# Node one-hots from broadcast key rows on ScalarE instead of TensorE, and layer-3 target scores made a block ahead, in a four-layer graph network

## The chip, the cores and the metric

The kernel runs on one core of one Trainium2 chip. The metric is the device time of one execution in microseconds. The core has a matrix engine (TensorE, PE in the profile, with its weight loads as PEld), two elementwise engines (VectorE, DVE; ScalarE, ACT), GpSimd (POOL), which here issues the indirect DMAs, and SyncE (SP), which issues the plain DMAs. Each engine works through its own queue in order; semaphores tie the queues together.

## The reference, cut to what matters

6250 nodes with 256 features, 100000 edges sorted by target. Four graph layers follow each other, each added to its input and normalised over the features:

```python
edge_index = jnp.stack([src, dst])
x = _layernorm(x + _L0_gnn_ref(x, edge_index, ...))     # mean of neighbours, two matrices
x = _layernorm(x + _L1_gnn_ref(x, src, dst, ...))       # attention, 8 heads: q[row] . k[col], softmax per source
x = _layernorm(x + _L2_gnn_ref(x, edge_index, ...))     # two GAT layers, 4 heads
x = _layernorm(x + _L3_gnn_ref(x, edge_index, ...))     # mean of neighbours, two matrices
```

The attention layer and the GAT layer are the two that the change touches:

```python
s = jnp.einsum('ehd,ehd->eh', q[row], k[col])
p = jnp.exp(s - m[row])
out = jax.ops.segment_sum((p / denom[row])[:, :, None] * v[col], row, num_segments=n)
...
e = jax.nn.leaky_relu(alpha_s[src] + alpha_d[dst], 0.2)
ex = jnp.exp(e - m[dst])
out = jax.ops.segment_sum(h[src] * alpha[:, :, None], dst, num_segments=n)
```

`q[row]`, `alpha_d[dst]` take a node's row out to its edges, and `segment_sum` brings the edges' rows back to their node. Both are matrix products with one-hot matrices: a node-by-edge hot to go out, an edge-by-node hot to come back.

## The kernel before, in words

The nodes are cut into NB = 50 blocks of B = 125. For each block the edges whose target (or source, in the attention layer) lies in it are laid out in CM = 16 chunks of 128 edges (CAP = 2048 in all); what doesn't fit goes to SH = 2 chunks that 25 blocks share. `key_d` and `key_s` hold for each edge its node's number inside its block, one column a chunk; `idx_d` and `idx_s` hold the other end.

The program has a preparation (to about 200 us) and five passes over the blocks. Pass 1 is the first layer and, beside it, the sort by source. Pass 2 is the attention layer (`piece1`, `finish1`), passes 3 and 4 are the two GAT layers (`piece2`, `finish2` with `layer` 0 and 1), pass 5 is the last layer. Beside passes 3 and 4 `count_edges` builds a table of edge counts for pass 5, one step after most turns.

A block is worked through in four pieces of four chunks, 200 pieces a pass. A piece is a Python generator that issues some instructions and yields the name of a group. `Turns` steps the generators: in each turn it goes through the groups in a fixed order and steps every item of that group that is due; `yield "x"` makes it due in the next turn, `yield "+x"` in this one, if that group is still to come. This order is the order of the instructions in the queues of PE, DVE and ACT. POOL and SP are not ordered by hand.

Pass 2, a piece: gathers of four chunks of `kv_table` into `g` (7 buffers), POOL. Then "tp": TensorE makes both hots. `by_node` and `by_key` are factors of 56 rows whose product is 1 minus the squared distance of node and key; four products give `t_t` (node by edge), one gives `t_s` (edge by node), both in the bank `tp`. Then "act": ScalarE evicts them through a Relu, to `ts` in bf16 (L1873) and to `st` in f32 (L977, `positive`). Then "qe" (L1882): `ts` times the three bf16 parts of the block's `q` gives each edge its query. Then "prod" (L1889): keys times queries on DVE, a reduction `s` (L1821), and two Exp on ACT (L1825 to `iota_p`, L1826 to `msg`). Then "msg" (L1828): values times weights on DVE. Then "ps" (L1908): `st` times `msg` is summed in the block's bank. After its last piece a block goes through `finish1`: the division, two small transposes and a product (L915, L920, L928), the layer norm (`norm`, L898) and `features`, which multiplies by the GAT weights, stores a row of `hs_table` for each node and keeps the target's score in three bf16 parts, `ad_parts`.

Passes 3 and 4, a piece: gathers of `hs_table` into `g` (9 buffers), POOL; DVE makes the edge-by-node hot `st` by comparison (`one_hots`, L941). "tp": TensorE transposes it (L2085). "act": ScalarE evicts it to `ts` in bf16 (L2088). "pe": `ts` times `ad_parts` of the block gives each edge its target's score, into the one bank `pe` (L2093). "e": the sum `e` (L2049) and the leaky ReLU `r` (L2043) on DVE, two Exp on ACT (L2052, L2053). "msg" (L2055) and "ps" (L2127) as before. `finish2` does the division, Gelu (L2011, another activation table than Exp), then `features` for the next GAT layer, or the norm and the tables of pass 5.

The counting step k makes a hot `a_hot` on DVE (L1965), multiplies that of step k-1 on TensorE into the one bank `a_acc` (L1975) and lets ScalarE evict that of step k-2 to `a_row` (L1951).

## Time and profile before

| what | value |
|---|---|
| median of 3 runs (lowest, highest) | 6354.93 us (6344.74, 6355.41) |
| the profiled execution's own time | 6347.38 us |
| its span on the core | 6345.5 us |
| PE busy in 1410 to 2790 us (pass 2) | 1037.08 of 1380 us |
| PE busy in 2790 to 4160 us (pass 3) | 1028.08 of 1370 us |
| PE busy in 4160 to 5560 us (pass 4) | 957.16 of 1400 us |
| ACT busy in the same three stretches | 386.43, 450.35, 492.35 us |
| POOL busy in the same three stretches | 767.78, 778.13, 757.95 us |

A group of the profile is named by its line, engine, operation and tiles, with its number of instructions, its busy time, the mean length of one, and the idle time of the engine just before it with what ended that idle time. Three passes of 1380, 1370 and 1400 us make two thirds of the span; the change lies in these. The rows of the groups that it takes away, from the groups by shape:

```profile
L2085 PE MATMUL tp<-ident,st 128*125 128x128 f32 x1600 | 308.5, 314 | 40.6 <-issue 30.1 <-DVE st L941 10.1
L2088 ACT CAST ts<-tp 125x512 bf16<-125x512 f32 x400 | 233.3, 583 | 820.7 <-remote 479.2 <-PE tp L2085 164.0 <-PE pe L2093 135.6
L1873 ACT ACTIVATE ts<-tp 125x512 bf16<-125x512 f32 x200 | 118.4, 592 | 258.5 <-PE fin L970 108.1 <-remote 86.4 <-PE tp L1869 37.7
L977 ACT ACTIVATE st<-tp 128x500 f32<-128x500 f32 x200 | 116.5, 582 | 4.6 <-PE tp L970 1.5 <-PE tp L1869 1.4 <-PE qe L1882 0.8
L1869 PE MATMUL tp<-by_key,by_node 56*128 56x128 bf16 x800 | 81.2, 224 | 7.9 <-ACT ts L1873 6.8 <-ACT by_key L966 0.8 <-issue 0.3
L970 PE MATMUL tp<-by_node,by_key 56*128 56x500 bf16 x200 | 78.3, 392 | 22.8 <-ACT by_key L966 18.3 <-issue 4.2 <-ACT st L977 0.2
```

### The profile page before, as it was taken

To read this page: it belongs to the slowest core of one execution; us is meant where nothing else is said; L and a number is where in the kernel's file an instruction comes from. 1 tells how busy PE (TensorE), PEld (TensorE's weight loads), DVE (VectorE), ACT (ScalarE), POOL (GpSimd) and SP (SyncE) were. 2 spreads that over 40 slices of the span, in tenths; PEclk is the share of its full clock that TensorE was granted. 3 is DMA by queue.
4 is the path that set the end of the run, shared out by engine and by line. 5 is a ranking of instruction groups with operands and counts; after the bars stand their busy time and mean duration, and the time that the engine had idled before them with its cause. 6 is when DMAs were issued, how large, how long until landed. Compare 5 with 4: busy or idle time off the path is not lost.

```text
span 6345.5 us, 85961 instructions
## 1 busy us (share of the span) xinstructions
PE 4651.2 (73%) x28778; PEld 3328.7 (52%) x28778; DVE 3995.7 (63%) x11239; ACT 2312.8 (36%) x6308; POOL 3590.8 (57%) x3709
## 2 busy tenths in 40 slices
PE   1567888867777777757777777747766776779996
PEld 0445666645555555535555555535545555545554
DVE  7786666646777777746666666646767767623233
ACT  4016677932322222213333333323333333323332
POOL 5776666645555555535555555455555555455554
PEclk9778999988999999978888888878888878889997
DMA  5555555545655556533333333333333333377774
GB/s 152 152 163 157 160 157 151 153 129 170 177 173 171 172 167 174 171 86 96 105 102 102 102 101 101 90 83 102 104 100 104 105 102 97 93 189 206 205 193 122
DMA packets 383758, 862.39 MB, mean 136 GB/s; under 512 B 85018, under 2 KB 208376, under 8 KB 383304
## 3 DMA queue, kind: packets, MB, share of 16 engines
q0 software_dynamic: 221184, 670.83, 39.0%
q1 hardware_dynamic: 162120, 185.97, 10.2%
q8 instruction: 228, 3.74, 0.2%
q14 instruction: 226, 1.85, 0.1%
HBM read 769.69 MB, written 86.78 MB: 135 GB/s over the span
## 4 chain that ended last, share of the span: by engine, by line
PE 35%; DVE 22%; issue 13%; another core or an unknown queue 10%; ACT 9%; POOL 5%; DMA 3%; SPq 0%; DVEq 0%; ACTq 0%; POOLq 0%
PE ps L2127 6%; PE d L2274 6%; POOL g L932 5%; PE ps L985 5%; PE a_acc L1975 4%; DVE msg L2055 3%; PE po L928 2%; DVE s L1821 2%; PE tp L2085 2%; DVE msg L1828 2%; PE acc L1519 2%; DVE a_hot L1965 2%; DMA g<-kv_table_f,idx_s 2%; PE pt L928 2%
## 5 line engine op out<-in xcount | busy, mean ns | idle before, releaser
L932 POOL DMA_INDIRECT g<-hs_table_f,idx_d x1600 | 1520.9, 951 | 1249.8 <-DVE msg L2055 493.8
L932 POOL DMA_INDIRECT g<-kv_table_f,idx_s x784 | 746.7, 952 | 548.9 <-issue 204.2
L932 POOL DMA_INDIRECT g<-h_table_f,idx_d x800 | 799.5, 999 | 430.6 <-issue 213.8
L2127 PE MATMUL ps<-msg,st 128*125 128x260 f32 x3200 | 919.6, 434 | 97.2 <-DVE msg L2055 52.9
L2127 PEld LDWEIGHTS ps<-msg,st 128*125 128x125 f32 x3200 | 688.5, 218 | 291.6 <-issue 82.8
L1975 PE MATMUL a_acc<-a_hot,a_st 128*128 128x500 f16 x1650 | 497.6, 444 | 373.6 <-ACT a_row L1951 282.8
L2055 DVE TENSOR_TENSOR msg<-g,iota_p 128x1024 f32<-128x1024 f32 x400 | 488.2, 1221 | 403.6 <-ACT iota_p L2052 328.0
L932 POOL DMA_INDIRECT g<-x_table_f,idx_d x416 | 395.7, 951 | 383.4 <-PE ps L985 191.4
L985 PE MATMUL ps<-g,st 128*128 128x256 bf16 (+1 forms) x3648 | 519.3, 293 | 126.1 <-issue 60.4
L985 PEld LDWEIGHTS <-st 128*128 128x128 bf16 x4104 | 419.2, 104 | 255.8 <-issue 150.3
L2088 ACT CAST ts<-tp 125x512 bf16<-125x512 f32 x400 | 233.3, 583 | 820.7 <-remote 479.2
L1965 DVE TENSOR_SCALAR a_hot<-a_nodes,a_ends 128x500 f16<-128x500 f16 x1650 | 505.2, 372 | 18.1 <-remote 18.1
L1908 PE MATMUL ps<-msg,st 128*125 128x264 f32 x1600 | 437.7, 419 | 100.6 <-DVE msg L1828 73.3
L1975 PEld LDWEIGHTS <-a_st 128*128 128x128 f16 x1650 | 180.5, 109 | 577.1 <-issue 484.6
L1908 PEld LDWEIGHTS ps<-msg,st 128*125 128x125 f32 x1600 | 301.4, 199 | 237.3 <-DVE msg L1828 103.9
L941 DVE TENSOR_TENSOR st<-iota_p,key_d 128x500 f32<-128x500 f32 (+1 forms) x550 | 409.8, 746 | 20.8 <-ACT iota_p L2052 16.3
L2274 PE MATMUL d<-cnt,xs 125*128 125x500 bf16 x1800 | 401.2, 378 | 16.9 <-issue 16.5
L1889 DVE TENSOR_TENSOR prod<-g,qe 128x512 f32<-128x512 f32 x400 | 262.3, 684 | 197.5 <-PE qe L1882 68.3
L2049 DVE TENSOR_TENSOR e<-g,pe 128x16 f32<-128x16 f32 x400 | 65.1, 163 | 454.7 <-remote 352.1
L1882 PE MATMUL qe<-q,ts 125*128 125x256 bf16 x2400 | 318.9, 286 | 29.0 <-DVE prod L1889 24.2
L2085 PE MATMUL tp<-ident,st 128*125 128x128 f32 x1600 | 308.5, 314 | 40.6 <-issue 30.1
L1532 ACT ACTIVATE oa<-t_f,blk 125x128 f16<-125x128 f16 x800 | 310.7, 388 | 74.4 <-remote 48.1
(453 smaller groups left out, 8768.0 us busy)
## 6 DMA issues: line engine op xcount, KB each, us to landing
g<-hs_table_f,idx_d POOLq DMA_INDIRECT x1600
xs<-x_table_f SPq DMA_DIRECT2D x75, 336.0 KB
a_table_f<-a_row SPq DMA_DIRECT2D x50, 328.1 KB
few<-a_table_f SPq DMA_DIRECT2D x75, 218.8 KB
g<-h_table_f,idx_d POOLq DMA_INDIRECT x800
g<-kv_table_f,idx_s POOLq DMA_INDIRECT x784
hs_table_f<-hs SPq DMA_DIRECT2D x100, 115.5 KB
own<-hs_table_f SPq DMA_DIRECT2D x100, 115.5 KB
```

The costliest lines, as they stand in the source:

```text
L932: nc.gpsimd.indirect_dma_start(out=g, out_offset=None, in_=table, in_offset=bass.IndirectOffsetOnAxis(ap=idx, axis=0))
L941: nc.vector.tensor_tensor(st, iota_p[:, None, :w].to_broadcast([P, n, w]), key[:, :, None].to_broadcast([P, n, w]), op=ALU.is_equal,)
L985: nc.tensor.matmul(ps[:, :m], st[:, i, :], g[:, i, k * D : k * D + m], start=(c0 + i == 0 and k == 2), stop=(c0 + i == CH - 1 and k == 0),)
L1532: nc.scalar.activation(oa[:, i, :], o1[:, i, :], AF.Copy, scale=val_a[:, at])
L1882: nc.tensor.matmul(qe[:, i, :], ts[:, i0 + i, :], q[:, k * D : (k + 1) * D], start=(k == 0), stop=(k == 2))
L1908: nc.tensor.matmul(sums[b][:B, : D + H1], hot, m[:, i * H1 : (i + 1) * H1, :].rearrange("p h c -> p (h c)"), start=(c == 0), stop=(c == CH ...
L1965: nc.vector.tensor_scalar(hots[k][:, i, :], nodes, ends[:, s, c : c + 1], float(-r * RW), op0=ALU.subtract, op1=ALU.is_equal,)
L1975: nc.tensor.matmul(accs[s, r], sts[s][:, c, :], hot[:, i, :], start=(c == c0), stop=(c == c1 - 1))
L2055: nc.vector.tensor_mul(msg[:, : n * H2, :C2].rearrange("p (n h) c -> p n h c", h=H2), g[:, :n, :D].rearrange("p n (h c) -> p n h c", h=H2) ...
L2085: nc.tensor.transpose(tp[:, i, :], st[:, i, :], ident)
L2127: nc.tensor.matmul(sums[b][:B, : D + H2], hot, m[:, i * H2 : (i + 1) * H2, :].rearrange("p h c -> p (h c)"), start=False, stop=(c == CH - 1),)
L2274: nc.tensor.matmul(accs[h][q], xs[:, i, j * D + h * P : j * D + (h + 1) * P], cnt[:, i, q * RW : (q + 1) * RW], start=(s + i == 0 and j == 2),
```

## The change

Key rows: the preparation and the sort by source store the keys of each block as one row of 2048 bf16 numbers in DRAM, `keys_d` and `keys_s`. In passes 2 to 4 SP loads a block's row to all 125 partitions at once (`load_keys`, three buffers), six turns ahead of the block's first piece. From three turns ahead ScalarE turns it into the node-by-edge hot where it lies, a quarter a turn: Square with minus the partition's number as bias, then Relu of 1 minus that (`node_hots`). So `by_node`, `by_key`, their products, the transposes `tp` and the copies `ts` go.

Pass 2's edge-by-node hot is made by ScalarE too (`edge_hots`): a Square for each chunk, with the key as bias, and one Relu for the piece, when the piece is made. In passes 3 and 4 it stays with VectorE.

Passes 3 and 4: the scores of a block's targets are made for the whole block, with the hots, into one of two banks `pe`; the piece only reads them. A piece takes two stages fewer. The order of the groups changes, `run_pass` also adds the key generators, `qe` gets four banks, `ps` three in pass 2, `g` six buffers in passes 2 to 4, and the counting gets a step more between its product and its eviction, with a third `a_hot` and a second `a_acc`.

```diff
+        minus = const.tile([P, 1], F32, name="minus")
+        nc.gpsimd.iota(minus, pattern=[[1, 1]], base=0, channel_multiplier=-1, allow_small_or_imprecise_dtypes=True)
...
+        keys_d, keys_s = (dram.tile([NB, CAP], BF16, name=f"keys_{k}_f") for k in "ds")
...
+        def node_hots(kb, q):
+
+            part = kb[:, q * 4 * P : (q + 1) * 4 * P]
+            nc.scalar.activation(part, part, AF.Square, bias=minus[:B])
+            nc.scalar.activation(part, part, AF.Relu, bias=ones[:B, 0:1], scale=-1.0)
+
+        def edge_hots(work, key, n, most, bufs, name):
+
+            st = work.tile([P, most, B], F32, name=name, bufs=bufs)[:, :n, :]
             for i in range(n):
...
+                nc.scalar.activation(st[:, i, :], iota[:, :B], AF.Square, bias=key[:, i : i + 1], scale=-1.0)
+            nc.scalar.activation(st, st, AF.Relu, bias=ones[:, 0:1], scale=-1.0)
             return st
...
+            k_rows = pool.tile([NB, CAP], BF16, name="k_rows")
+            nc.scalar.copy(k_rows, k_f)
+            nc.sync.dma_start(out=keys_d, in_=k_rows)
...
+        LEAD_K = 6
+
+        def run_pass(turns, makers, beside=None, keys=None):
...
             for t, make in enumerate(makers):
+                if keys and (t + LEAD_K) % per == 0 and 2 <= (t + LEAD_K) // per < NB:
+                    turns.add(keys((t + LEAD_K) // per))
                 turns.add(make())
...
+        def load_keys(rows, b):
+            kb = keys_pool.tile([B, CAP], BF16, name="kb")
+            move(nc.sync, kb, rows[b : b + 1, :].to_broadcast([B, CAP]))
+            return kb
...
-            turns = Turns(("act", "prod", "msg", "fin", "ps", "late", "qe", "tp", "new"))
+            turns = Turns(("late", "keys", "qe", "prod", "msg", "fin", "ps", "new", "act"))
...
+            def keys1(b):
+                kb = load_keys(keys_s, b)
+                held[b] = work.tile([B, 3 * D], BF16, name="q", bufs=3)
+                move(nc.sync, held[b], block_rows(q_table, b))
+                by_key[b] = kb.rearrange("p (c e) -> p c e", e=P)
+                yield "3keys"
+                for q in range(CM // 4):
+                    node_hots(kb, q)
+                    yield "keys"
...
-                yield "tp"
-                ks = by_key[b]
-                t_t, t_s = (psum.tile([P, 512], F32, name="tp", bufs=2) for _ in range(2))
-                for i in range(n):
-                    nc.tensor.matmul(t_t[:, i * P : (i + 1) * P], by_node[:, c0 + i, :], ks, start=True, stop=True)
-                hots_product(t_s, by_node, ks, c0, n)
-                yield "act"
-                ts = work.tile([B, 4, P], BF16, name="ts", bufs=3)
-                nc.scalar.activation(ts[:, :n, :].rearrange("p c e -> p (c e)"), t_t[:B, : n * P], AF.Relu)
-                st = positive(work, t_s, n, 4, 5, "st")
+                st = edge_hots(work, key_s[:, b, c0 : c0 + n], n, 4, 6, "st")
+                if last:
+                    st_s = edge_hots(work, key_s[:, b, CM:], SH, SH, 2, "st_s")
                 yield "qe"
...
-            for k in range(len(steps) + 2):
-                if k >= 2:
-                    s, r = steps[k - 2]
+            for k in range(len(steps) + 3):
+                if k >= 3:
+                    s, r = steps[k - 3]
...
-                    hots[k] = ap.tile([P, most, RW], F16, name="a_hot", bufs=2)
+                    hots[k] = ap.tile([P, most, RW], F16, name="a_hot", bufs=3)
...
-                    accs[s, r] = apsum.tile([P, 512], F32, name="a_acc")[:, :RW]
+                    accs[s, r] = apsum.tile([P, 512], F32, name="a_acc", bufs=2)[:, :RW]
...
-                turns = Turns(("act", "e", "msg", "fin", "ps", "late", "pe", "tp", "new"))
+                turns = Turns(("late", "keys", "e", "pe", "msg", "fin", "ps", "new", "act"))
...
+                def keys2(b):
+                    kb = load_keys(keys_d, b)
+                    yield "3keys"
+                    ts = kb.rearrange("p (c e) -> p c e", e=P)
+                    pe = scores_d[b] = psum.tile([P, CM, H2], F32, name="pe", bufs=2)
+                    for q in range(CM // 4):
+                        node_hots(kb, q)
+                        yield "+pe"
+                        for c in range(4 * q, 4 * q + 4):
+                            for k in range(3):
+                                nc.tensor.matmul(
+                                    pe[:, c, :], ts[:, c, :], ad_parts[:, b, k, :], start=(k == 0), stop=(k == 2)
+                                )
+                        yield "keys"
...
-                    st = one_hots(work, key_d[:, b, c0 : c0 + n], n, 4, 8)
-                    yield "tp"
-                    tp = psum.tile([B, 4, P], F32, name="tp", bufs=2)
-                    for i in range(n):
-                        nc.tensor.transpose(tp[:, i, :], st[:, i, :], ident)
-                    yield "act"
-                    ts = work.tile([B, 4, P], BF16, name="ts", bufs=3)
-                    nc.scalar.copy(ts[:, :n, :], tp[:, :n, :])
-                    yield "pe"
...
+                    st = one_hots(work, key_d[:, b, c0 : c0 + n], n, 4, 6)
+                    yield "2e"
+                    pe = scores_d[b][:, c0 : c0 + n, :]
...
-                    run_pass(turns, [(lambda a=a: piece2(*a)) for a in made], beside_2)
+                    run_pass(turns, [(lambda a=a: piece2(*a)) for a in made], beside_2, keys2)
```

A digit ahead of a group's name, as in "3keys", means that many turns later. `finish1`, `finish2` and `features` keep their instructions in the new groups: the layer products of a block come first in a turn ("late"), ScalarE's copies of them last ("act"); `features` in pass 2 uses the block's own bank in place of a bank `fin`. The generator for the shared chunks waits five turns in place of four.

## The prediction

> **What bounds the kernel now.** I read the page's busy line first, then busy time by stretch (PE, PEld, DVE, ACT, POOL busy; clock; DMA share; GB/s), because the change touches passes 2 to 4 only. One steady stretch of each:
>
> ```profile
> PE 4651.2 (73%) x28778; PEld 3328.7 (52%) x28778; DVE 3995.7 (63%) x11239; ACT 2312.8 (36%) x6308; POOL 3590.8 (57%) x3709
> ...
> 1600.00:2600.00 1000.00, 768.08 (x4458) 553.35 (x4456) 744.64 (x1449) 291.49 (x823) 575.52 (x605) 0.96 0.59 171
> 3000.00:4000.00 1000.00, 784.30 (x4877) 566.00 (x4877) 658.93 (x1803) 346.31 (x956) 584.55 (x616) 0.87 0.38 102
> 4360.00:5360.00 1000.00, 699.44 (x4462) 515.36 (x4461) 696.91 (x1999) 364.49 (x967) 551.70 (x581) 0.83 0.37 102
> ```
>
> No engine is full: the busiest, PE, idles a fifth to a third of the time. So the engines wait for one another. The waits by stretch (waiting line, releaser, us, times, longest) say where; these are pass 2, then pass 3:
>
> ```profile
> DVE msg L1828 <- issue: 57.0, 84, 2.1
> DVE msg L1828 <- ACT iota_p L1825: 46.6, 66, 3.0
> DVE prod L1889 <- PE qe L1882: 44.8, 34, 3.9
> DVE prod L1889 <- PE tp L970: 22.9, 18, 1.4
> ACT ts L1873 <- PE fin L970: 94.6, 21, 4.9
> ```
>
> ```profile
> DVE msg L2055 <- ACT iota_p L2052: 149.1, 101, 3.7
> DVE e L2049 <- remote: 114.6, 35, 8.0
> ACT ts L2088 <- remote: 194.7, 35, 12.3
> ACT ts L2088 <- PE pe L2093: 90.6, 18, 7.5
> PE a_acc L1975 <- ACT a_row L1951: 84.1, 62, 3.9
> POOL g L932 <- DVE msg L2055: 196.5, 69, 5.9
> ```
>
> (The last two are from 2900 to 4100 us.) VectorE waits for TensorE's products and for ScalarE's exponentials, and ScalarE's exponentials stand behind copies of one-hots that wait for TensorE. "remote" ahead of `ts` and `e` I take for TensorE as well: nothing but TensorE feeds `ts`, and some matmul records are missing. POOL is held back by VectorE, not the reverse. A stretch of the timeline of pass 3 shows the knot:
>
> ```profile
> 3614.82 0.10 PEld L2093 LDWEIGHTS <-ts 125*128 125x128 bf16 x1
> 3616.11 0.15 DVE L2049 TENSOR_TENSOR e<-g,pe 128x16 f32<-128x16 f32 x1
> 3616.32 0.44 PE L2093 MATMUL pe<-ad_parts,ts 125*128 125x4 bf16 x12 [1.11 <-DVE e L2049]
> 3616.60 0.51 PEld L2085 LDWEIGHTS tp<-ident,st 128*125 128x125 f32 x4
> ```
>
> `pe` has one buffer, so the next piece's `pe` waits for `e`, and the transposes `tp` stand behind it.
>
> **What the Trainium skill says.** "TensorE: Matmul & The Clock Gate", Step-by-step: what each phase is for: matmuls stay in program order, only weight loads are pulled ahead. The trace agrees: the load of `ts` at 3614.82 ran 1.5 us before its matmul. "ScalarE: Activation LUTs", What ACT_TABLE_LOAD costs: 186 + 0.833 N ns for an ACTIVATE, about 93 more for each per-partition operand, neighbours overlapping by about 93. The trace agrees: one such operand on 128 elements took 388 ns (L1532; 280 + 107), two on 256 took 600 ns (L898; 585). Same page, Table sets: cheap functions lie in every set; Square is not in that list, though Precision budgets groups it with relu and identity. No run here shows Square yet.
>
> **The turn as unit.** 200 pieces make 200 turns a pass. From first to last issue of one line: pass 2, L1882, 1425.4 to 2773.7, 6.78 us a turn; pass 3, L2127, 2846.5 to 4132.7, 6.46; pass 4, 4212 to 5561.8, 6.78. Floors: VectorE's work a turn is share times turn: 0.745 x 6.78 = 5.05 us; 0.659 x 6.46 = 4.26; 0.697 x 6.78 = 4.73. POOL's is 4 gathers of 0.95 us + 0.30 us of issue = 5.0.
>
> **What goes from TensorE.** Pass 2: L1869 81.2 us, L970's `tp` 78.3, its `st_s` and the turning of key rows some 15 (an estimate from 50 matmuls of 0.28 us): 175 us, 0.9 a turn. Passes 3 and 4: L2085, 308.5 us, 0.77 a turn. None counts in full, TensorE being not the bound; it counts as waits that end.
>
> **What ScalarE gains and loses.** Out: two evictions of 592 and 582 ns a piece in pass 2 (118 + 117 us), `ts` 583 ns in passes 3 and 4 (233 us). In, every pass: eight operations on 125x512 bf16 a block, 186 + 93 + 426 = 705 ns, 0.61 apart with overlap: 1.2 us a turn, 245 us a pass. In pass 2 also four Squares on 125 elements (383 ns, 0.29 apart) and one Relu on 500 (696, 0.60): 1.8 us a turn, and 1.0 more a block for the shared chunk: 400 us. Pass 2's ScalarE rises from about 2.0 to 0.7 + 1.2 + 2.0 = 3.9 us a turn, passes 3 and 4 from 2.2 to 2.9 and from 2.5 to 3.1. These are the lower ends; without any overlap it is 4.7, 3.1 and 3.3.
>
> **Pass 2.** After the change no hot waits for TensorE, `qe` is made a turn ahead in four banks, so the waits of `prod` go: 44.8 + 22.9 and, from the same view, 13.6 <- PE fin, 10.5 <- remote, 15.8 <- issue: 108 us in 1000. Waits of `msg` for the exponential are 104, of which 0.33 x 148 turns = 49 must stay (the exponential lies between `s` and `msg`); 55 could go. What comes instead: the instruction behind which the hots now queue. In the turn of the layer norm ScalarE's `x_sb` waits until the norm's chain on VectorE ends (4.8 us idle ahead of it in the timeline); then 0.6 + hots 1.8 + 1.0 + next block's node hots 1.2 = 4.6 us lie ahead of the next exponential, while VectorE needs 1.28 + 1.22 = 2.5 us to ask for it: about 2.1 us a block, 80 us in 1000. Net 83 in 1000, 0.56 a turn: 6.2. Ends: 5.4 (VectorE's floor and 0.33) and 6.8. 200 x 0.58 = 116 us.
>
> **Pass 3.** `tp`, `ts` and the single `pe` go from the piece; the scores come a block ahead into two banks, so `e` waits for nothing of its own block: 114.6 + 15.7 (a_acc) + 11.6 (ps) + 3.8 = 146 us in 1000 go. Of the 169 us that `msg` waits, 0.31 x 155 = 48 and a table load of 1.28 us x 38 blocks = 49 stay; 72 go. All of it would give 0.78 x 6.46 = 5.05 a turn, which is POOL's 5.0 as well. Two engines at one floor, tied by six buffers in place of nine, will not both be full: I take 5.7; ends 5.05 and 6.46. 200 x 0.76 = 152 us. The six buffers cost nothing of themselves: a piece holds one from its gather to `msg`, three turns instead of five, so the slack falls from three turns to two, 11 us against 5 us of gathering.
>
> **Pass 4.** `e` 109.3 + 20.1 + 12.2 = 142 go, of `msg`'s 134 all but 96; the norm's `x_sb` and `xp` ahead of node hots give back 0.7 us a block (ScalarE 3.0 us against VectorE's 2.3): net 155 in 1000, 5.7 a turn at best; I take 6.0. 200 x 0.78 = 156 us.
>
> **Edits with one answer.** The groups' new order puts the late products ahead of `qe` and `ps` on TensorE and ScalarE's copies last in the turn, after the exponential; layer products reuse their block's own bank, so `sums` has three: no cost, each operand being ready a turn before. Counting: another `a_hot`, another `a_acc` bank, a step's more lag: this ends L1975's waits for `a_row` (282.8 us in all), which are inside what I counted. `node_factors` and the first `key_factors` at the start of pass 2 go: two VectorE operations of 2.5 us and a dozen small, 10 us before the first product. Two turns fewer of filling and draining a pass, ends only: 20 us in all, 0 to 60 (there are idle stretches of 31 and 35 us at the starts of passes 3 and 4 that I can't explain and don't count). New in passes 0 and 1: one copy of 2048 (1.9 us), seven transposes, copies and stores of key rows beside the gathers: 5 us, 0 to 10. New DMA: 512 KB a block from SP into three buffers, asked for six turns ahead, used from three turns ahead; `q` moves with it: four issues of 0.3 to 0.4 us a block on SP, whose wait for a free buffer (block b-3's, read last two turns before) would hold only stores of `hs`, which the next pass needs at its end. Pass 2's gathers move 190.6 MB in 55.3% of 16 engines over 1200 us, 287 GB/s, so 1.8 us of the DMA engines in 25: share 0.59 to 0.72 at the faster pace, and late only if a load takes over 17 us.
>
> **Sum.** 116 + 152 + 156 + 10 + 20 - 5 = 449 us from the profiled execution's 6347.4 (span 6345.5 and 1.9 around it): 5898. The median of the runs shown lies 7.5 above; 5900 is my number.
>
> **Rivals.** (1) ScalarE in order takes more back: without overlap a turn of pass 2 has 4.5 us of ScalarE between two exponentials against VectorE's 4.05 (`prod`, `s`, 0.33, `msg`), and the norm turn's stall is 3.0; that is 0.56 a turn more, all of pass 2's gain; passes 3 and 4 keep half of theirs. Gain 5 + 76 + 78 + 25 = 184: 6160. For it: the exponential already ends most of VectorE's waits. Against: ScalarE is 29 to 36% busy. (2) The waits called remote are not the chain that is cut, but gathers landing or TensorE itself stalling: then only `prod`'s waits and the pass 2 start go, some 60 us: 6290. For it: the unexplained idle at the starts; against: `ts` reads nothing that a gather writes. (3) Every wait that can go goes, and POOL and VectorE set the pace: 5.9, 5.05 and 5.7 a turn, gain 176 + 282 + 216 + 25 = 699: 5650. (4) Slower: Square shares no set with Exp. Place: ScalarE, between the hots and every exponential. Price: a load of 1283 ns in each turn, where only one turn in four of passes 3 and 4 has one now: 1.28 x 200 in pass 2, 1.28 x 50 more there in the norm's turns, 1.28 x 150 in passes 3 and 4 each, 704 us against the gain of 449: 6600. It decides from 449 / 600 = 0.75 us a turn ahead of the exponential, which is 350 loads; late key rows could cost as much there, but nothing in the DMA shares speaks for it.
>
> **Chances.** Forecast 0.52, (1) 0.22, (2) 0.06, (3) 0.05, (4) and what acts at its place 0.15. The forecast's own range is 5750 to 6020; taking in (1) gives 5700 to 6310 for 8 in 10. A measurement of this kernel can tell 0.2% (13 us) from no change. Faster 0.81: forecast, (1), (3) and a third of (2); same 0.03; slower 0.16.
>
> **What would show it.** Right: no `tp` and no `ts` row; L1889 and `e` with idle under 50 us each; ACT busy near 800 us in pass 2; about 200 table loads; POOL's share up to 62% or more; turns of 6.2, 5.7, 6.0. Wrong: `msg` waiting for ACT over 200 us in pass 2 (rival 1), `e` still waiting over 200 us (rival 2), table loads by the hundred (rival 4), or node hots waiting for key rows.

## The result and the profile after

The change makes the kernel slower: 6785.89 us (6780.25 to 6795.57) against 6354.56 us (four executions; the three ahead of the prediction gave 6354.93), ratio 1.0684 with an interval of 1.0666 to 1.0703. The forecast was 5900, 0.928 of before.

First the busy line and three groups of the page of the changed kernel, then its busy time by stretch in passes 2, 3 and 4 (columns as before: PE, PEld, DVE, ACT, POOL busy, clock, DMA share, GB/s):

```profile
PE 4624.1 (68%) x26085; PEld 3171.6 (47%) x26085; DVE 3957.2 (58%) x11174; ACT 3088.6 (46%) x7786; POOL 3574.8 (53%) x3710
...
L899 POOL DMA_INDIRECT g<-hs_table_f,idx_d x1600 | 1516.9, 948 | 1513.1 <-DVE msg L2024 949.4
L2097 PE MATMUL ps<-msg,st 128*125 128x260 f32 x3200 | 1055.9, 470 | 183.4 <-issue 172.5
...
L1973 DVE TENSOR_SCALAR rdens<-ps 125x4 f32<-125x4 f32 x100 | 16.2, 162 | 806.2 <-remote 468.7
```

```profile
1600.00:2600.00 1000.00, 675.41 (x3147) 486.58 (x3145) 631.22 (x1206) 542.78 (x1414) 492.46 (x521) 0.79 0.57 165
3100.00:4100.00 1000.00, 657.68 (x3719) 430.79 (x3717) 571.82 (x1576) 414.62 (x963) 512.85 (x541) 0.76 0.39 106
4700.00:5700.00 1000.00, 681.19 (x3656) 443.12 (x3655) 645.90 (x1866) 450.61 (x1041) 514.35 (x544) 0.76 0.41 112
```

2693 instructions fewer on TensorE take only 27 us less, every other engine but ScalarE does less in 1000 us than before, and the granted clock fell in pass 3 from 0.87 to 0.76. Nothing is fuller; something stalls. VectorE's waits of the changed kernel (waiting line, releaser, us, times, longest) in pass 2 (1421 to 2962 us) and in pass 3 (3001 to 4450 us) say where:

```profile
DVE prod L1871 <- remote: 218.0, 41, 8.4
DVE msg L1811 <- ACT iota_p L1808: 140.5, 120, 3.0
DVE prod L1871 <- DMA g<-kv_table_f,idx_s: 109.4, 36, 7.9
```

```profile
DVE rdens L1973 <- remote: 254.1, 26, 12.3
DVE rdens L1973 <- PE ps L2097: 104.2, 10, 12.4
DVE msg L2024 <- ACT iota_p L2021: 85.3, 75, 5.2
...
DVE rdens L1973 <- PE a_acc L1945: 55.3, 6, 10.1
DVE rdens L1973 <- PE pe L2050: 54.6, 5, 12.1
...
DVE e L2018 <- remote: 4.0, 1, 4.0
```

In pass 3 `e` waits no more, as foretold, but once a block `rdens`, the first reader of a block's sum, waits about 10 us: 468 us in all. The timeline of the changed kernel shows one such wait:

```profile
3615.22 0.18 PEld L2097 LDWEIGHTS ps<-msg_s,st_s 128*125 128x125 f32 x1 [1.22 <-issue]
...
3616.61 0.38 PE L2097 MATMUL ps<-msg_s,st_s 128*125 128x260 f32 x1 [1.71 <-issue]
...
3618.02 0.59 PE L2097 MATMUL ps<-msg_s,st_s 128*125 128x260 f32 x1 [1.03 <-issue]
...
3619.63 0.95 POOL L899 DMA_INDIRECT g<-hs_table_f,idx_d  x1 [0.30 <-issue]
...
3620.84 0.58 PE L1945 MATMUL a_acc<-a_hot,a_st 128*128 128x500 f16 x1 [0.83 <-issue]
...
3626.46 0.57 PE L1945 MATMUL a_acc<-a_hot,a_st 128*128 128x500 f16 x1 [1.54 <-issue]
...
3627.53 0.16 DVE L1973 TENSOR_SCALAR rdens<-ps 125x4 f32<-125x4 f32 x1 [10.09 <-PE a_acc L1945]
3627.56 0.51 PE L2050 MATMUL pe<-ad_parts,kb 125*128 125x4 bf16 x12
...
3634.23 0.94 POOL L899 DMA_INDIRECT g<-hs_table_f,idx_d  x1 [9.90 <-DVE msg L2024]
```

From 3615 to 3627 us TensorE waits for nothing the profile shows ("issue"), yet begins one instruction, load or matmul, each 0.7 us or at multiples of it; at 3627.56 it does twelve products in 0.51 us. Meanwhile GpSimd issues one gather each 1.25 us without a pause until 3624.3. The slow stretch ends 2 to 3 us after that. Then VectorE catches up: `msg` begins at 3632.7, 3635.1, 3640.1 and 3645.2, four pieces in less time than the 5 us a piece that GpSimd needs to gather them. So from 3634 on GpSimd finds four buffers free in succession and gathers 16 times without a pause, and from 3644 on TensorE is slow again. This repeats in most blocks.

The granted clock is not the cause. In this stretch, which begins at 3613.8, it stays at full until 3618.0, is half until 3631.6, and so follows the slow stretch in and out by about 4 us.

Two countings over the records carry the rest. For the first, TensorE instructions (loads and matmuls) that begin less than 0.55 us after the one before them are taken together with it; a *slow stretch* is four or more successive starts that then lie 0.55 to 3 us apart. A *run* is a number of gathers with less than 0.6 us between them. Before has 56 slow stretches, 323 us; after has 148, 1210 us. (The sums that the expectations below quote, some 360 and 1326 us, come from a slightly wider counting.) In passes 2 to 4, of the runs of each length, so many have a slow stretch begin in them or before the next run; a few longer runs at the starts of the passes are left out:

| gathers in the run | before | after |
|---|---|---|
| 4 | 0 of 177 | 1 of 115 |
| 8 | 16 of 170 | 7 of 17 |
| 12 | 9 of 16 | 67 of 79 |
| 16 | 1 of 2 | 43 of 44 |

The stretch begins about 9 us (passes 3 and 4) or 12 us (pass 2) into the run.

One place in the same two executions does not fit. In pass 1 the gathers of `h_table` follow each other each 1.4 us, not 1.25, and there runs of 26, 38 and 54 of them (before) and of 32, 38 and 42 (after), 37 to 75 us long, have no slow stretch at all. (The first run of the pass has some, and has them in the unslowed place too.) For instance, the run of 54 of before (columns as above):

```profile
361.00:436.00 75.00, 51.39 (x280) 38.82 (x280) 62.57 (x98) 10.19 (x35) 58.85 (x54) 0.80 0.61 166
```

So a long run is not enough by itself; the pace of the gathers may count too. No run tests this.

By passes, from the first to the last `msg` (199 turns), in us a turn (the prediction measured by other lines: 6.78, 6.46 and 6.78): the recorded pair, the same two kernels in another series of runs (next section), and kernels of the experiments:

| kernel | pass 2 | pass 3 | pass 4 |
|---|---|---|---|
| before, recorded | 6.66 | 6.48 | 6.85 |
| after, recorded | 7.63 | 7.46 | 7.47 |
| before, unslowed place | 5.95 | 5.05 | 5.84 |
| after, unslowed place | 5.98 | 5.06 | 5.72 |
| exponentials behind `msg`, unslowed place | 5.47 | 5.06 | 5.08 |
| the same and a pause each 4 gathers, slowed place | 6.29 | 6.06 | 6.03 |
| before and a pause each 4 gathers, slowed place | 6.55 | 6.17 | 6.46 |

The three passes take 192, 195 and 123 us more than before, 511 together; the gaps between them take 65 us less (67.6 and 64.0 before, 36.3 and 30.3 after), the start of pass 2 comes 4.4 us earlier and the end from pass 4 on takes the same. That is the 441 us between the spans of 6345.5 and 6786.3.

### The profile page after: what moved, and what is told of

Same layout as the page of the kernel before. It is cut to its first block, busy times and chain, and to the rows that moved or that the text cites. A ratio compares the mean times of both kernels' runs of the same rounds, so it can differ in the third digit from the quotient of the medians.

```text
span 6786.3 us, 82224 instructions
## 1 busy us (share of the span) xinstructions
PE 4624.1 (68%) x26085; PEld 3171.6 (47%) x26085; DVE 3957.2 (58%) x11174; ACT 3088.6 (46%) x7786; POOL 3574.8 (53%) x3710
## 3 DMA queue, kind: packets, MB, share of 16 engines
q0 software_dynamic: 221184, 670.83, 36.7%
## 4 chain that ended last, share of the span: by engine, by line
PE 29%; DVE 24%; issue 16%; ACT 14%; another core or an unknown queue 9%; POOL 5%; DMA 2%; DVEq 0%; SPq 0%; ACTq 0%; POOLq 0%
PE ps L2097 7%; PE d L2244 5%; POOL g L899 5%; PE ps L933 4%; PE a_acc L1945 3%; DVE a_hot L1935 2%; DVE msg L2024 2%; PE po L895 2%; DVE msg L1811 2%; ACT kb L918 2%; ACT kb L917 2%; PE acc L1470 2%; DVE st L908 1%; DMA g<-kv_table_f,idx_s 1%
## 5 line engine op out<-in xcount | busy, mean ns | idle before, releaser
L2097 PE MATMUL ps<-msg,st 128*125 128x260 f32 x3200 | 1055.9, 470 | 183.4 <-issue 172.5
L2097 PEld LDWEIGHTS ps<-msg,st 128*125 128x125 f32 x3200 | 709.4, 231 | 379.5 <-issue 250.5
L1945 PE MATMUL a_acc<-a_hot,a_st 128*128 128x500 f16 x1650 | 523.9, 451 | 387.7 <-ACT a_row L1921 232.9
L1881 PE MATMUL ps<-msg,st 128*125 128x264 f32 x1600 | 491.0, 435 | 135.3 <-issue 128.0
L1973 DVE TENSOR_SCALAR rdens<-ps 125x4 f32<-125x4 f32 x100 | 16.2, 162 | 806.2 <-remote 468.7
L2050 PE MATMUL pe<-ad_parts,kb 125*128 125x4 bf16 x4800 | 211.1, 166 | 357.9 <-issue 275.5
L918 ACT ACTIVATE kb<-kb,ones 125x512 bf16<-125x512 bf16 x600 | 432.4, 721 | 19.0
L1881 PEld LDWEIGHTS ps<-msg,st 128*125 128x125 f32 x1600 | 324.7, 214 | 239.9 <-issue 180.3
L917 ACT ACTIVATE kb<-kb,minus 125x512 bf16<-125x512 bf16 x600 | 428.8, 715 | 5.3 <-DMA kb<-keys_d_f 4.0
L2050 PEld LDWEIGHTS <-kb 125*128 125x128 bf16 x4800 | 197.2, 100 | 480.0 <-issue 335.4
```

Source lines behind the costliest of these rows:

```text
L917: nc.scalar.activation(part, part, AF.Square, bias=minus[:B])
L918: nc.scalar.activation(part, part, AF.Relu, bias=ones[:B, 0:1], scale=-1.0)
L1881: nc.tensor.matmul(sums[b][:B, : D + H1], hot, m[:, i * H1 : (i + 1) * H1, :].rearrange("p h c -> p (h c)"), start=(c == 0), stop=(c == CH ...
L1945: nc.tensor.matmul(accs[s, r], sts[s][:, c, :], hot[:, i, :], start=(c == c0), stop=(c == c1 - 1))
L2050: nc.tensor.matmul(pe[:, c, :], ts[:, c, :], ad_parts[:, b, k, :], start=(k == 0), stop=(k == 2))
L2097: nc.tensor.matmul(sums[b][:B, : D + H2], hot, m[:, i * H2 : (i + 1) * H2, :].rearrange("p h c -> p (h c)"), start=False, stop=(c == CH - 1),)
```

## The experiments

**Where it was run decides.** The same kernel before ran at 5436 to 5449 us in some series and at 6348 to 6458 in others, the recorded pair among these. Here the first are called the unslowed place, the second the slowed one. Of the place only the chip's number is on record; two chips (1 and 6) were met both ways, so it is not the chip alone. What makes a place slow stays open. The DMAs are not slower there: in the traces of before the gathers of `hs_table` land 2.45 us after their issue in either place (median, from the packets of their queue; at most 4.3), and a packet of 4096 bytes takes 226 and 227 ns. Every ratio below is to runs of the kernel before on the same chip in the same series.

**The unchanged kernels, unslowed place.** No edit. 

> The changed kernel, nothing edited, once more. In the runs so far the kernel before took 6354 us in one place and 5449 in another, and a variant of the changed kernel had 1326 us of slow TensorE stretches in the first place and some 85 in the second. Theory A (the slow stretches decide, and they come and go with where the program runs): where the kernel before takes about 5450, the changed one takes 5400 to 5440, ratio 0.99 to 1.0, with under 150 us of slow stretches; where it takes about 6350, the changed one takes about 6790 again. Theory D (what was lost is ScalarE's and VectorE's waiting, wherever it runs): ratio 1.05 or more in both places.

After: 5410.25 against 5442.02, ratio 0.9946 (0.9929 to 0.9962). 

> The kernel before, nothing edited, for its trace in this place. Theory A: its slow TensorE stretches are under 100 us in sum where it takes about 5450, and its turns are 5.5 to 6 us in passes 2 to 4; some 360 us and 6.5 to 6.8 a turn where it takes about 6350. Theory D: its turns are shorter than those of the changed kernel in either place.

Before: 5435.33. The slow stretches are 77 us before and 93 after, none of them in passes 2 to 4, though in pass 3 of both kernels GpSimd gathers 808 times in one run. So in this place even the longest run does no harm. The waits in pass 2 (1280 to 2460 us) of before, then of after:

```profile
DVE prod L1889 <- PE qe L1882: 92.2, 92, 3.3
DVE msg L1828 <- ACT iota_p L1825: 64.7, 193, 0.8
```

```profile
DVE msg L1811 <- ACT iota_p L1808: 165.6, 192, 2.9
DVE prod L1871 <- PE qe L1863: 15.8, 9, 4.2
```

What `prod` gains (76 us) `msg` gives back waiting for ScalarE (101 us). In pass 3 both kernels go at GpSimd's pace, 5.05 us a turn. So the change, apart from the slowing, is worth half a per cent.

**Pauses between the gathers.** First try: five small iotas on POOL after each piece's gathers.

```diff
+        def pause():
+            for _ in range(5):
+                nc.gpsimd.iota(diff, pattern=[[1, P]], base=0, channel_multiplier=-1, allow_small_or_imprecise_dtypes=True)
```

> The changed kernel with five small iotas (0.24 us each by the trace) on POOL after each piece's four gathers in passes 2 to 4; nothing else differs. Theory A (bursts of gathers): TensorE falls to about one instruction in 0.7 us once POOL has gathered for 8 to 11 us without a pause, as it does once a block in passes 2 and 3 of the changed kernel; with a pause of about 1.2 us after every 5 us the slow stretches shrink from about 1200 us in passes 2 to 4 to under 400, and the time falls below 6500 although POOL gets 1.2 us a turn more to do. Theory B (TensorE's own load: it is slowed after running full for some 10 us, whatever POOL does): slow stretches stay once a block, 6790 or more. Theory C (six buffers are too few, gathers come late): later gathers, slower, 6850 to 7050.

6264.46 against 5449.18, 1.15 (1.1479 to 1.1522). Nothing tied the iotas to the gathers, so nearly 2600 of the 3000 ran ahead of pass 2 and held up the work there (pass 2 began at 2033 us, not at 1285). The run tells nothing of the theories.

Second try: a memset of the gather buffer itself, about 1 us, which must run between the buffer's release and its gathers. This is the edit in pass 2, then in passes 3 and 4:

```diff
                 g = gp.tile([P, 4, 2 * D], F32, name="g")
+                nc.gpsimd.memset(g[:, 0:2, :], 0.0)
...
                     g = gp.tile([P, 4, D + 8], F32, name="g")
+                    nc.gpsimd.memset(g, 0.0)
```

> The changed kernel with a memset of 1024 to 1056 f32 columns on POOL ahead of each piece's gathers, into the buffer that they fill, so that it stays in its place (the iotas of the first pause had no place of their own and ran during passes 0 and 1). About 1 us a turn. Theory A: where the changed kernel is slow (about 6790), runs of gathers are broken and the slow stretches shrink by half or more, time below 6550; where it is at about 5430, the pause only costs: POOL has 6.0 us a turn against turns of 6.0 and 5.45, 50 to 250 us more. Theory D: slower than the changed kernel in both places.

5679.86 against 5442.02, 1.0436 (1.0418 to 1.0455), in the unslowed place: the pauses' price where there is nothing to cure, 270 us more than the changed kernel alone.

**Four buffers in place of six.**

```diff
-        with tc.tile_pool(name="f1g", bufs=6) as gp, ...
+        with tc.tile_pool(name="f1g", bufs=4) as gp, ...
```

(and the same in `f2g`.) 

> The changed kernel with four gather buffers a pass in place of six (passes 2 to 4). Theory A: after a stall only four pieces can be caught up at once, so runs of gathers are shorter; slow stretches fall by a third or more, time 6400 to 6700. Theory B: slow stretches stay, 6790 to 6900. Theory C: too few buffers become fewer, 6900 to 7300.

5418.82 against 5449.18, 0.9946 (0.9928 to 0.9964), turns of 5.95, 5.08 and 5.72: as with six. Too few buffers are not what limits it there. This run met the unslowed place; in the slowed one, where it would bear on the theories, it was not tried.

**TensorE beside one thing at a time.** Behind the kernel, five stretches of 200 float32 products each (the profile counts each as two matmuls): alone, beside 36 gathers, beside 36 gathers with an iota after every fourth, beside 36 plain transfers from SP, beside 36 iotas.

```diff
+            for part in range(5):
+                if part in (1, 2):
+                    for j in range(NGA):
+                        gather(mg[:, j, :], hs_tables[1][:, :], mi[:, j : j + 1])
+                        if part == 2 and j % 4 == 3:
+                            nc.gpsimd.iota(ml, pattern=[[1, 1200]], ...)
+                if part == 3:
+                    for j in range(NGA):
+                        nc.sync.dma_start(out=mg[:, j, :], in_=hs_tables[1][j * P : (j + 1) * P, :])
+                if part == 4:
+                    for j in range(36):
+                        nc.gpsimd.iota(ml, pattern=[[1, 1200]], ...)
+                for j in range(NM):
+                    nc.tensor.matmul(mp[:B, :D], mw[:, j % 2, :B], mw[:, 1 - j % 2, :], ...)
```

> The changed kernel, and behind its last pass five stretches of 200 f32 matmuls 125x125 by 125x256, each with its own weight load, one stretch after the other: (0) alone, (1) beside 36 gathers of 128 rows of 1056 bytes without a pause, (2) beside the same with a pause of about 1.2 us after every four, (3) beside 36 plain transfers of 128 rows of 1056 bytes issued by SP, (4) beside 36 iotas on POOL. About 0.24 us a matmul where nothing slows it, 48 us a stretch. Theory A: (1) alone is slow from its eighth to eleventh us on, at about 0.7 us an instruction until the gathers end at about 45 us, so that far fewer matmuls are done by then; (2) is slower than (0) by a quarter or less; (3) and (4) say whether the transfers or POOL at work do it, and I expect neither alone. Theory B: all five are slow after some 10 us, (0) too. Theory C says nothing of it: all five equal, at 48 us.

> The five stretches of 200 f32 matmuls once more, beside nothing, unbroken gathers, gathers in fours with pauses, plain transfers, and POOL at work. The first time all five ran alike, at 0.22 us for each of the two halves of a matmul, about 87 us a stretch. Theory A: where the kernel before takes about 6350, the stretch beside unbroken gathers is slowed from its tenth us or so on, by 20 us or more, and the first and last are not; where it takes 5450, all are alike again. Theory B (TensorE's own load): the first is slowed as well. Theory D: all alike in both places.

Both met the unslowed place (5859.68 and 5865.16) and all five stretches took 87 to 90 us. The third time, behind the reordered kernel told of below, it met the slowed place:

> The kernel e6_order, and behind its last pass the five stretches of 200 f32 matmuls of e1_apart (alone, beside 36 unbroken gathers, beside gathers in fours with pauses, beside plain transfers, beside iotas on POOL), which add some 450 us. Where TensorE is slowed (before at about 6350 to 6430): theory A (unbroken gathers set off the slow stretches): the stretch beside unbroken gathers takes 20 us or more longer than the 87 us of the first one, slowed from its seventh to eleventh us until the gathers end; beside gathers with pauses less than half of that; the other three are not slowed. Theory B (TensorE's own load): the first is slowed as well. In the passes ahead, where GpSimd gathers without a break, theory A expects slow stretches in every pass and 6300 or more for all of it. Where TensorE is not slowed (before at 5440): about 5640, all five stretches alike.

6999.91 against 6356.46. The iotas again did not stay in place: they ran beside the first stretch, and the third is unbroken gathers like the second. Busy time by stretch: beside iotas; beside gathers, their first 19 us; the next 31 us; after the gathers; beside plain transfers; alone:

```profile
6486.00:6574.00 88.00, 88.00 (x399) 76.19 (x400) 9.52 (x3) 0.00 (x0) 49.49 (x44) 0.98 0.00 1
6576.00:6595.00 19.00, 19.00 (x89) 16.31 (x88) 0.00 (x0) 0.00 (x0) 14.32 (x16) 1.00 0.37 101
6595.00:6626.00 31.00, 9.28 (x19) 4.53 (x19) 0.18 (x1) 0.00 (x0) 19.85 (x21) 0.57 0.35 96
6627.00:6680.00 53.00, 53.00 (x240) 45.82 (x239) 0.00 (x0) 0.00 (x0) 0.00 (x0) 0.97 0.00 1
6811.00:6890.00 79.00, 79.00 (x368) 68.66 (x366) 0.01 (x1) 0.00 (x0) 0.00 (x0) 1.00 0.22 62
6900.00:6984.00 84.00, 84.00 (x391) 73.02 (x390) 0.00 (x0) 0.00 (x0) 0.00 (x0) 1.00 0.00 1
```

and in the unslowed place, the same 31 us beside gathers (`e2_apart`):

```profile
5516.00:5547.00 31.00, 31.00 (x146) 26.99 (x145) 0.00 (x0) 0.00 (x0) 23.10 (x25) 1.00 0.41 109
```

19 matmuls against 146, with nothing else at work but the gathers and with inputs that were all ready. The slowing begins 19 us after the first gather and ends some 6 us after the last; the third stretch, with unbroken gathers too, repeats it (118 us in place of 87). Here as well the clock follows. The first 4 us of the slow part, at full clock, already have only 6 matmuls; then come 28 us at half clock:

```profile
6595.00:6599.00 4.00, 1.48 (x6) 0.92 (x5) 0.00 (x0) 0.00 (x0) 3.08 (x4) 1.00 0.37 101
6599.00:6627.00 28.00, 8.68 (x16) 4.18 (x15) 0.18 (x1) 0.00 (x0) 16.76 (x18) 0.50 0.34 92
```

GpSimd's own computing (45 iotas, 50 us) does not do it, nor does TensorE's own load. Plain transfers did not do it either, at up to 288 GB/s against 101 for the gathers, but they were over after some 19 us, when the gathers had only begun to tell; longer ones were not tried.

**Fewer gathers in a run.** In passes 3 and 4 the fourth gather of each piece becomes a plain transfer of other rows.

```diff
-                        gather(g[:, i, :], table[:, :], idx_d[:, b, c0 + i : c0 + i + 1])
+                        if i < 3:
+                            gather(g[:, i, :], table[:, :], idx_d[:, b, c0 + i : c0 + i + 1])
+                        else:
+                            nc.sync.dma_start(out=g[:, i, :], in_=table[:P, :])
```

> The changed kernel with the fourth gather of each piece in passes 3 and 4 replaced by a plain transfer of 128 fixed rows of the table, issued by SP; the bytes stay, GpSimd has three gathers a piece in place of four, 3.75 us a turn in place of 5.0. The scores of that chunk are of other nodes than the edges name. Where TensorE is not slowed (changed kernel 5410, passes 3 and 4 from 2506 to 4680): theory E (GpSimd's pace of 5.0 us a turn holds pass 3, where it idles only 0.3 us between gathers): from 2510 to 3550 its unbroken row of gathers ends and pass 3 gets 40 to 120 us shorter, bound by VectorE (853 us busy in 1040) after that; pass 4 changes by under 40. Rival F (pass 3 is held by VectorE's waits for ScalarE): under 20 us in both. Where TensorE is slowed (before at about 6350): theory A expects far fewer slow stretches in passes 3 and 4, with runs of gathers of 4 us, and 6300 or less.

Slowed place: 6143.36 against 6430.28, one execution each. Pass 2, untouched, took 7.77 us a turn, passes 3 and 4 took 5.54 and 5.91, where the recorded run of after took 7.46 and 7.47. A quarter less work for GpSimd mixes into this, so the next runs keep all gathers.

**Pauses in the slowed place.** The changed kernel with the memsets, and stretches behind it, twice:

> The kernel e2_pause (the changed kernel with a memset of about 1 us ahead of each piece's gathers in passes 2 to 4), and behind its last pass five stretches of 200 f32 matmuls, 87 us where nothing slows them: (0) alone, (1) beside 36 unbroken gathers, (2) beside gathers in fours, each four followed by one POOL copy of 720 columns, (3) beside 36 plain transfers of the same size, (4) beside gathers in fours, each followed by three such copies. The stretches add some 450 us. Where TensorE is slowed (before at 6350 to 6430): theory A: (1) takes 117 us or so, slowed from about its twentieth us until the gathers end; (2) less, (4) least, under 95; and in passes 2 to 4 the slow stretches of the changed kernel (about 1100 us there) shrink by half or more, so that the whole is under 7000, where the changed kernel and the stretches would take about 7290. If pauses don't help, the rate of gathers isn't what counts, and 7350 or more comes out. Where TensorE is not slowed (before at 5440): all stretches 87 to 90, about 6130 in all.

> e9_pause again, which met a place where TensorE is not slowed (before 5436, this 6134, as expected there). Where it is slowed (before at 6350 to 6430): theory A: the stretch beside unbroken gathers takes about 117 us, that in fours with one copy less, that with three copies under 95; slow stretches in passes 2 to 4 at half of the changed kernel's or less, the whole under 7000. If pauses don't help: 7350 or more. Elsewhere: 6134 again.

The first met the unslowed place (6133.9 against 5436.36), the second the slowed one: 6450.45 against 6348.37 with the stretches, which begin at 5896.7 us. The passes are done by then and a last step of some 10 us follows the stretches, so the kernel itself comes to about 5905 (one execution). Its passes take 6.09, 6.02 and 6.03 us a turn, where after took 7.63, 7.46 and 7.47. A slow stretch begins in 3 of its 574 runs of four and in 2 of its 16 runs of eight. Passes 2 and 3 of that run by stretch, and the memsets' group:

```profile
1600.00:2500.00 900.00, 687.84 (x3642) 533.89 (x3643) 732.82 (x1397) 627.38 (x1636) 720.51 (x756) 0.90 0.75 212
2750.00:3750.00 1000.00, 742.10 (x4580) 510.36 (x4580) 815.96 (x1928) 508.96 (x1192) 798.82 (x831) 0.85 0.48 132
```

```profile
L2063 POOL MEMSET g<- 128x1056 f32 x400 | 397.4, 995 | 73.6 <-DMA hs_table_f<-hs 53.3 <-DMA w_r<-in_L_gnn_W_r 20.2
```

A microsecond of other work on GpSimd between each four gathers and the next, some 590 us of added work, makes the kernel some 880 us shorter. The pause does two things at once: it breaks the runs, and over several pieces it holds GpSimd to one gather each 1.5 us where 1.25 was possible. These runs do not tell the two apart. (The copies meant to break the gathers of the added stretches did not stay between them; all three stretches beside gathers took 117 to 118 us against 87.)

**What ScalarE's work costs, unslowed place.** Hots left out: `node_hots` does nothing (keys scaled by 1e-4 when stored), `edge_hots` gives a constant.

```diff
-            nc.scalar.activation(part, part, AF.Square, bias=minus[:B])
-            nc.scalar.activation(part, part, AF.Relu, bias=ones[:B, 0:1], scale=-1.0)
+            pass
...
-                st = edge_hots(work, key_s[:, b, c0 : c0 + n], n, 4, 6, "st")
+                st = st_s = same
```

> The changed kernel with ScalarE's one-hots left out: node hots in passes 2 to 4 (the key rows, scaled to 0.0001 of their value, stand in for them) and edge hots in pass 2 (one constant tile stands in). Every transfer, matmul and VectorE operation stays. It prices what ScalarE's part costs where TensorE is not slowed (changed kernel 5410, before 5442; pass 2 from 1272 to 2467, passes 3 and 4 from 2506 to 4680). Theory E (what TensorE's part gave back is taken by ScalarE ahead of the exponential in pass 2, while GpSimd at 5.0 us a turn bounds pass 3 and VectorE pass 4): pass 2 ends 80 to 150 us sooner, msg's waits for ScalarE in it fall from 166 to under 80 us in 1180, passes 3 and 4 change by under 50 us together. Theory F (pass 2 is held by GpSimd and VectorE as well): under 40 us in pass 2.

5270.62 against 5442.72; turns of 5.39, 5.08, 5.52. `msg` waits 63.6 us for the exponential in 1280 to 2400 us, near the 64.7 of before. So the hots cost pass 2 about 0.59 us a turn, 118 us, pass 3 nothing and pass 4 0.2 us a turn, 40 us (one execution).

Pass 2's node hots on VectorE, by one comparison:

```diff
-                    node_hots(kb, q)
+                    node_hots_v(kb, q)   # nc.vector.tensor_scalar(part, part, pidx[:B], None, op0=ALU.is_equal)
```

> The changed kernel with pass 2's node hots made by VectorE: one comparison with the partition's number on 125x512 bf16 a turn, about 0.4 us by a_hot's 0.37 us for 500 columns, in place of ScalarE's Square and Relu, 0.72 us each. Where TensorE is not slowed (changed kernel 5410, before 5442): theory E (ScalarE ahead of the exponential holds pass 2, and leaving all hots out took 106 us off it): pass 2 gets 40 to 90 us shorter, msg's waits for ScalarE in it fall from 166 us to under 110, time 5320 to 5370, ratio 0.977 to 0.987. Rival F (VectorE is as near to its floor as ScalarE is in the way): its 80 us more of work come in full, ratio 1.0 to 1.01. Where TensorE is slowed (before at about 6350): theory A, which takes the slow stretches as set off by long unbroken runs of gathers, expects 6700 to 6850, their number unchanged.

5381.39 against 5439.29, 0.9893 (0.9874 to 0.9912), a little short of the gain expected; pass 2 takes 5.83 us a turn, and `msg` still waits 86.9 us.

**Which exponential `msg` waits for.** `weights_p`, in PSUM, is one tile for all factors, and in the records of the changed kernel `msg` begins just after the exponential of the *next* piece has ended: before the 51st `msg`, 52 are done. In one kernel `msg` reads its factors from the gathered message's own last column, so that the first exponential goes:

```diff
-                pp = weights_p[:, 4 * H1 * k : 4 * H1 * (k + 1)]
-                nc.scalar.activation(pp[:, : n * H1], s[:, : n * H1], AF.Exp)
...
+                    msg[:, : n * H1, C1:].rearrange("p (n h) c -> p n h c", h=H1).to_broadcast([P, n, H1, C1]),
```

> The changed kernel with one exponential a piece left out: msg on VectorE takes its factors from the last column of its own buffer, where the second exponential writes them anyway, and no longer from weights_p in PSUM. Theory G (msg waits for the exponential of the next piece, because the exponentials of all pieces write one PSUM tile: in the trace 52 exponentials are done before the 51st msg, and it starts 0.21 to 0.25 us after the latest): msg's waits for ScalarE fall from 166 us in 1180 of pass 2 to under 50, and likewise in pass 4; the time falls by 60 to 200 us against the changed kernel, ratio to before 0.96 to 0.985. Rival H (msg waits for its own exponential, which is only due then): nothing but 0.2 us of ScalarE a turn goes, within 25 us of the changed kernel, ratio 0.99 to 0.998. Where TensorE is slowed (before at 6350) both leave it above 6650.

5435.43 against 5442.72, 0.9991 (0.9977 to 1.0005). The wait goes, as theory G has it, but the time does not follow. Two groups of this kernel, then the gathers' group of the changed one in an unslowed place:

```profile
L899 POOL DMA_INDIRECT g<-hs_table_f,idx_d x1600 | 1693.6, 1058 | 559.8 <-issue 424.8 <-DMA kb<-keys_d_f 55.5 <-DVE a_hot L1933 21.6
...
L2020 DVE TENSOR_TENSOR msg<-g,msg 128x1024 f32<-128x1024 f32 x400 | 488.5, 1221 | 13.3 <-ACT msg L2018 13.3
```

```profile
L899 POOL DMA_INDIRECT g<-hs_table_f,idx_d x1600 | 1522.0, 951 | 690.5 <-issue 406.1 <-DVE msg L2024 144.4 <-DMA kb<-keys_d_f 57.5
```

In passes 3 and 4 13.3 us of the wait are left, but both inputs of `msg` lie in SBUF now and a gather takes 1058 ns in place of 951; pass 3, which goes at GpSimd's pace, takes 5.56 us a turn. The gain is given back.

The other way is the order: a group "exp" behind "msg", so that a turn's exponential is issued after the `msg` that must not wait for it (with the VectorE node hots of pass 2):

```diff
-            turns = Turns(("late", "keys", "qe", "prod", "msg", "fin", "ps", "new", "act"))
+            turns = Turns(("late", "keys", "qe", "prod", "msg", "exp", "fin", "ps", "new", "act"))
...
+                yield "+exp"
```

> The kernel e5_vector with the exponentials put behind msg in the order of a turn in passes 2 to 4, so that the msg of one piece no longer waits for the exponential of the next one, which writes the same PSUM tile (e4_own took that wait away by reading SBUF, and gathers went from 0.95 to 1.06 us each beside it). Where TensorE is not slowed (e5_vector 5381): theory G: msg's waits for ScalarE fall below 60 us in passes 2 and 4; pass 2 gets 60 to 120 us shorter, until GpSimd's 5.0 us a turn and VectorE's work bound it, pass 3 stays at GpSimd's pace, pass 4 gets 30 to 90 us shorter: 5180 to 5290, ratio 0.95 to 0.973. Rival I (each wait of VectorE that goes comes back as one for TensorE's products or for gathers, as in e4_own): 5350 or more. Where TensorE is slowed (before at about 6350): theory A expects the slow stretches to stay, 6500 or more.

5186.78 against 5444.56, 0.953 (0.9514 to 0.9546). In 1280 to 2300 us `msg` no longer stands among the waits, and those of `prod` are small:

```profile
DVE prod L1877 <- PE qe L1869: 12.7, 19, 1.8
DVE prod L1877 <- DMA g<-kv_table_f,idx_s: 9.9, 8, 2.7
```

In the slowed place this same kernel (before the stretches, above) comes to about 6495 us, against 6356 of before: without pauses it loses there too.

**How long a run may be, slowed place.** That kernel with the memset ahead of every second piece (runs of up to 8), and ahead of each piece (runs of 4):

> The kernel e6_order (exponentials behind msg, pass 2's node hots on VectorE) with the memset of about 1 us ahead of the gathers of every second piece in passes 2 to 4, so that at most eight gathers follow one another: GpSimd has 5.5 us a turn in place of 5.0. Theory A: where TensorE is slowed (before at about 6350, e6_order about 6490 there, the paused changed kernel about 5900): eight gathers are near the length from which stretches begin, so a few remain, under 300 us of them in passes 2 to 4, and the time is 5500 to 5800, below both kernels. Where it is not slowed (e6_order 5187, before 5440): GpSimd's pace rules, 5300 to 5420, at or below the kernel before. Rival: runs of eight are too long: 6000 or more in the slowed place.

6365.21 against 6352.54, 1.0022 (1.001 to 1.0034): theory A's 5500 to 5800 failed and the rival's 6000 or more came. A slow stretch begins in 52 of its 179 runs of 8, but also in 33 of 228 runs of 4: length is not all of it.

> The kernel e10_half with the memset of about 1 us ahead of the gathers of every piece in place of every second one: runs of four, GpSimd at 6.0 us a turn. Theory A: where TensorE is slowed (before at about 6350): stretches in passes 2 to 4 under 100 us as in e9_pause_2, three passes of 200 turns at 6.0 to 6.1 us, 5850 to 5950, ratio 0.92 to 0.94. Where it is not slowed (before at 5440): GpSimd's pace again, 5600 to 5680, ratio 1.03 to 1.045. Rival: eight gathers with one pause already were as slow as the kernel before, so four with one pause only looked free of stretches because the changed kernel runs more slowly between them: 6200 or more in the slowed place.

5984.06 against 6444.48, 0.9279 (0.9261 to 0.9297). The ratio is as expected, the time 34 us above the range; pass 2 takes 6.29 us a turn, the others 6.06 and 6.03. Slow stretches are 239 us in the whole kernel, 141 of them before pass 2.

**Pauses in the kernel before.** The two memsets and nothing else.

> The kernel before with the 1-us memset of the gather buffer ahead of each piece's four gathers in passes 2 to 4 and nothing else; its twin is the changed kernel with the same pauses. If this run meets the slowed place (the kernel before near 6350 to 6450): were the changed kernel's loss only the length of its gather runs, before too should gain from pauses, its passes running near 6.1 to 6.3, 6.05 and 6.1 us a turn, and end near 5950 to 6100, 0.93 to 0.96 of before; slow stretches of TensorE fall from some 360 us to under 250. The rival, that before doesn't suffer from its runs of 4 and 8 and loses its 900 us against the unslowed place otherwise, gives 6450 to 6650, slower than before by the pauses' price. If it meets the unslowed place (before near 5440), it can only give the price of the pauses: all passes near 6.03 to 6.1 a turn, 5690 to 5740, a ratio of 1.045 to 1.055, as the changed kernel with pauses gave 1.044.

Slowed place: 6155.84 against 6458.49, 0.9533 (0.9516 to 0.9549); slow stretches 217 us. Before suffers from its gathers too, though the turns of 6.55, 6.17 and 6.46 stay above those expected, and pass 2 hardly gains (6.66 as recorded). The gaps between the passes fall from 67.6 and 64.0 us as recorded to 38.8 and 34.7. With pauses the changed kernel stands at about 5905 / 6348 = 0.930, before at 0.953: about 2.5% between them, taken from two series.

## Why the prediction was wrong

**The step that failed first** is the reading of "remote": "'remote' ahead of `ts` and `e` I take for TensorE as well", and from it that those waits are "the chain that is cut". The sum took 424 us off the three passes for these waits; the passes took 511 more. It was TensorE, but for the most part TensorE slowed while GpSimd gathered, and not the chain of hots, `tp` and `pe`. Before, in the unslowed place, shows what the chain alone is worth: VectorE's waits in pass 3 (2510 to 3550 us) are

```profile
DVE msg L2055 <- ACT iota_p L2052: 107.6, 143, 1.8
DVE e L2049 <- issue: 17.9, 15, 3.9
DVE e L2049 <- DMA g<-hs_table_f,idx_d: 14.9, 12, 4.4
...
DVE e L2049 <- PE pe L2093: 3.8, 4, 2.1
```

so some 22 us of `e` in 1040 could go, not the 146 counted in 1000, and the pass already runs at 5.05 us a turn, the floor worked out for GpSimd. In pass 4 `e` waits 39.6 us for `pe` in 1030, where 142 in 1000 were counted. Only pass 2's count was near (`prod` for `qe` 92.2 in 1180, 78 in 1000, against 108), and that gain did come and went to `msg`. In the slowed place pass 3's wait moved from `e` to `rdens` (468 us in 1449).

What stalls before's own pass 2 there (6.66 against 5.95 us a turn) is not fully told: it has no slow stretch by the counting above. TensorE stops singly instead, as in 26 waits by "issue" of up to 1.4 us ahead of L915, 36 us in 1460 to 2450 us, where the unslowed run has none; and pauses hardly help this pass.

**The term that was missing** is what the gathers cost TensorE: it was put at nothing. "The six buffers cost nothing of themselves" counts slack in turns and does not ask how the buffers come free. VectorE now waits mostly once a block, catches up four pieces, and GpSimd gathers 12 or 16 times without a pause. The separate stretches show that gathers alone slow TensorE; the pauses show that breaking their runs, and with it slowing their pace, takes this away: 7.63, 7.46 and 7.47 become 6.09, 6.02 and 6.03 us a turn. That the runs are longer because of how VectorE waits is read from the timeline, not tried. Which part of the change makes them long (six buffers, the order of the groups, or the scores a block ahead) was not tried one by one in the slowed place.

**Rival (2)** held the mechanism, "TensorE itself stalling", at 0.06. Its time, 6290, came from leaving the stall as it was; that the change would lengthen it was in no case. The argument against it, "`ts` reads nothing that a gather writes", looked for a dependence of data, and the gathers need none: in the separate stretches the products read nothing that the gathers write. The idle 31 and 35 us that I could not explain were left uncounted, and were a sign of the stall. In the unslowed place the gaps between the passes of before are 36.7 and 30.1 us, as in the changed kernel there (36.1 and 30.3); in the slowed place they were 67.6 and 64.0. So the 65 us by which they shrank are not the "Two turns fewer", put at 20 (0 to 60).

**Rival (1)** is what happens in the unslowed place: ScalarE takes back pass 2's gain, which it put at "all of pass 2's gain". The reason was only half there: `msg` waits for the next piece's exponential, so whatever lies ahead of that one, hots included, delays this `msg`; the order kernel removes it. The 49 us in 1000 that "must stay" for `msg` need not.

**Rival (3)** did not come either, but its floor of 5.05 us for pass 3 is the pace of both kernels in the unslowed place, before as well as after.

**Rival (4)** fell. Square brought no table loads: 199 before and after. The Trainium skill, "ScalarE: Activation LUTs", Table sets, leaves Square out of its list of cheap functions; here it behaves as one of them. The rest of ScalarE was priced well: 715 and 721 ns for the hots against the 705 estimated from the same page's What ACT_TABLE_LOAD costs, 384 and 712 for Square and Relu of the edges against estimates of 383 and 696; busy in pass 2 of the unslowed run 813 us in 1180, at 5.98 a turn 4.1 us a turn against 3.9.

**Small, and near:** the start of pass 2 moved by 4 us recorded and 4 unslowed, where 10 less 5 was forecast; the key rows came in time, the DMA share in pass 2 rose from 0.66 to 0.73 in the unslowed place (forecast 0.59 to 0.72); neither `tp` nor `ts` is left.

## What to carry to other kernels

When a busy engine idles by "issue" or "remote" and its instructions start at equal distances, look at what another engine does at that moment before counting the idle time as a chain that an edit will cut. A change that only moves buffers' release can change the rhythm of a third engine; count runs of gathers and their pace, not only their sum. And a tile shared by turns ties a reader to its latest writer: put the writer behind the reader in the turn. Measure on more than one place before believing a few per cent.
